# The second node mix of a spectral layer moved in front of its second weight, and two layers in one set of pools

## Chip, cores and metric

The kernel runs on one core of one Trainium2 chip. The metric is the device time of one execution in microseconds. PE is TensorE, DVE VectorE, ACT ScalarE, POOL GpSimd, SP the engine that issues the DMAs.

## What is computed

Four graph layers in a row work on `x` of 128 graphs, 64 nodes and 256 features, all in f32. Each layer takes `h = relu(layernorm(x))` and adds its result to `x`. The first mixes nodes by a normalised adjacency and has two batch norms; the second is the one that is changed; the third multiplies by the adjacency twice and ends in short recurrences over windows of nodes (LSTMs); the fourth is attention along a list of edges. The second layer, with `U` the 64 eigenvectors of the graph's Laplacian, cut to what matters:

```
_, U = jnp.linalg.eigh(L_norm)
agg = jnp.einsum('mn,bnd->bmd', U.T, features)   # first node mix, 256 features
h = jax.nn.relu(agg @ W1 + b1)                   # 256 -> 128
out = h @ W2 + b2                                # 128 -> 256
return jnp.einsum('nm,bmd->bnd', U, out)         # second node mix
```

The front of the third layer:

```
h = relu(einsum('ts,bsh->bth', adj, x @ Wg0 + bg0))
h = relu(einsum('ts,bsh->bth', adj, h @ Wg1 + bg1))
```

## The kernel before

`x` stays in SBUF as 16 blocks `X[i]` of 512 rows (8 graphs), each 128 partitions by 4 tiles by 256 features; a partition is one node of one of two graphs. `eigenvectors` finds `U` while the first layer's products run beside it, and ends by making three 128x128 block-diagonal matrices: `BDA` from the adjacency, `BDU` from `U`, `BDUT` from its transpose. Each holds the matrix twice, for the two graphs of a tile. `mix` multiplies a block by such a matrix: the tile is the stationary operand and the matrix is moved past it, 128 columns at a time, so that the result comes out transposed (features on partitions). It goes to two PSUM banks.

`layer1` is the second layer (they are counted from 0). For each block `i` it first finishes the first layer for block `i + 2` (`end0`: batch norm on ACT, transposes by `ident` on PE, residual add on DVE) and takes the norm of block `i + 1` (`norm`: statistics on DVE, a square root on ACT, seven small DVE operations, four relus on ACT). Then come the first mix by `BDU`; its copy `a`, one half on DVE and one on ACT (`move` alternates); the first weight, with the weight stationary and `a` moving in 512 columns; a relu with bias on ACT into `z`; the second weight with `z` stationary and 256 columns moving; the bias on DVE into `y`; the second mix, `BDUT` stationary and `y` moving in 512 columns; and the residual add on DVE. The last three are done twice, for two tiles each.

`layer2` is the third layer. `adjacency_layers` loads two weights and makes small tables from the biases (`w2_rs`, `w2_B`, `w2_N`, and the second bias by way of `W1`), then does for each block the norm, a copy of `X[i]` out to memory (`spilled`), mix by `BDA`, first weight, a maximum with a table on DVE, second weight, bias, mix by `BDA` and relu. Ahead of block 2 it emits `edges`, the sorted edge tables of the fourth layer, held behind what had been emitted last on DVE, ACT and PE. `windows` then runs the recurrences.

Tiles come from pools. Each stage opens its own pools (`stage`), and a pool that takes over the place of a closed one waits for it (`reuse_waits`). The second layer has PSUM pools of 3, 3 and 2 banks, the third of 4 and 2, with 2 more for `edges`. The order of instructions on an engine is not that of the source: the framework puts them in order by its own plan, in which what is emitted first has precedence and what isn't ready is overtaken. So work of neighbouring blocks is interleaved. Nearly every instruction is recorded under line 799, where a helper (`Ordered`) issues it; rows are told apart by tile names.

Of the kernel before, what the change touches and what calls it, by code (L numbers as in the profile page):

```python
# [8 lines left out]
F32 = mybir.dt.float32  # L9
I32 = mybir.dt.int32  # L10
AF = mybir.ActivationFunctionType
ALU = mybir.AluOpType
AX = mybir.AxisListType
PSUM = bass.MemoryType.PSUM
# [1383 lines left out]
B, N, D = 128, 64, 256  # L1398
P = 128
NB = 16  # L1400
TPB = 4
BT = 512
E = 512
# [17 lines left out]
class Kernel:  # L1421
# [441 lines left out]
    def end0(self, i, psum):  # L1863

        sc2, sh2 = self.affine2
        for oc in range(2):
            self.act(self.part(i, oc), self.part(i, oc), AF.Identity, scale=sc2[:, oc:oc + 1], bias=sh2[:, oc:oc + 1])
        self.add_transposed(psum, i, lambda dc, j: self.part(i, dc)[:, j * P:(j + 1) * P])

    def layer1(self):
        o, io = self.o, self.io
        cx, (w, pool, psum, ps2, ps0) = self.stage([("l1w", 1), ("l1", 2), ("l1ps", 3), ("l1bps", 3), ("l1eps", 2)])
        with cx:
            W1 = self.weights(w, "w1_1", io["L1_gnn_W1"])
            W2 = self.weights(w, "w1_2", io["L1_gnn_W2"])
            b1 = self.columns(w, "w1_b1", io["L1_gnn_b1"])
            b2 = self.everywhere(w, "w1_b2", io["L1_gnn_b2"])

            self.end0(0, ps0)
            self.end0(1, ps0)
            hs = {0: self.norm(pool, 0)}
            for i in range(NB):
                if i + 2 < NB:
                    self.end0(i + 2, ps0)
                if i + 1 < NB:
                    hs[i + 1] = self.norm(pool, i + 1)
                h = hs.pop(i)
                a = pool.tile([P, 2, BT], F32, name="a")  # L1890
                self.mix(psum, h, self.BDU, lambda dc, p: self.move(a[:, dc, :], p[:]))
                p = psum.tile([P, BT], F32, name="ps")
                for kc in range(2):
                    self.mm(p[:], W1[:, kc, :], a[:, kc, :], kc == 0, kc == 1)
                z = pool.tile([P, BT], F32, name="z")
                self.act(z[:], p[:], AF.Relu, bias=b1[:, 0:1])
                for jj in range(0, TPB, 2):
                    p = ps2.tile([P, 2, D], F32, name="pt")
                    for j in range(2):
                        self.mm(p[:, j, :], z[:, (jj + j) * P:(jj + j + 1) * P], W2[:, 0, :])  # L1900
                    y = pool.tile([P, 2, D], F32, name="y")
                    o.add(y[:], p[:], b2[:, None, :].to_broadcast([P, 2, D]))
                    p = ps2.tile([P, 2, D], F32, name="pt")
                    self.mm(p[:].rearrange("p a b -> p (a b)"), self.BDUT[:], y[:].rearrange("p a b -> p (a b)"))
                    x = self.X[i][:, jj:jj + 2, :]
                    o.add(x, x, p[:])

    def layer2(self):  # L1910
        self.adjacency_layers()
        self.windows()

    def adjacency_layers(self):
        nc, o, io = self.nc, self.o, self.io
        cx, (w, pool, psum, ps2) = self.stage([("l2w", 1), ("l2", 2), ("l2ps", 4), ("l2bps", 2)])
        with cx:
            W0 = self.weights(w, "w2_0", io["L2_gnn_Wg0"])
            W1 = self.weights(w, "w2_1", io["L2_gnn_Wg1"])
            b0 = w.tile([1, D], F32, name="w2_b0")  # L1920
            nc.sync.dma_start(b0[:], io["L2_gnn_bg0"][None, :])
            b1 = self.everywhere(w, "w2_b1", io["L2_gnn_bg1"])


            rs = w.tile([1, P], F32, name="w2_rs")
            p = psum.tile([P, BT], F32, name="ps")
            for j in range(2):
                self.mm(p[0:1, j * N:(j + 1) * N], self.ones[:N, 0:1], self.AT[:])
            o.copy(rs[:], p[0:1, 0:P])
            B0, N0 = w.tile([P, 2, P], F32, name="w2_B"), w.tile([P, 2, N], F32, name="w2_N")  # L1930
            p = psum.tile([P, BT], F32, name="ps")
            for hc in range(2):
                self.mm(p[:, hc * P:(hc + 1) * P], b0[0:1, hc * P:(hc + 1) * P], rs[:])
            o.copy(B0[:], p[:, 0:2 * P].rearrange("p (h t) -> p h t", h=2))
            o.ts(N0[:], B0[:, :, 0:N], -1.0, ALU.mult)
            p = psum.tile([P, BT], F32, name="ps")
            for kc in range(2):
                self.mm(p[:, 0:D], B0[:, kc, :], W1[:, kc, :], kc == 0, kc == 1)
            o.add(b1[:], b1[:], p[:, 0:D])
            for i in range(NB):  # L1940
                if i == 2:
                    with ExitStack() as ce:
                        epool = ce.enter_context(self.tc.tile_pool(name="l3e", bufs=1, side="right"))
                        epsum = ce.enter_context(self.tc.tile_pool(name="l3eps", bufs=1, space=PSUM))
                        nc.vector.hold, nc.scalar.hold, nc.tensor.hold = nc.vector.last, nc.scalar.last, nc.tensor.last
                        self.edges(self.w3, epool, epsum)
                        nc.vector.hold = nc.scalar.hold = nc.tensor.hold = None
                h = self.norm(pool, i)
                nc.sync.dma_start(self.spilled(i), self.X[i][:])
                a = pool.tile([P, 2, BT], F32, name="a")  # L1950
                self.mix(psum, h, self.BDA, lambda dc, p: self.move(a[:, dc, :], p[:]))
                g = pool.tile([P, 2, BT], F32, name="g")
                for hc in range(2):
                    p = psum.tile([P, BT], F32, name="ps")
                    for kc in range(2):
                        self.mm(p[:], W0[:, kc, hc * P:(hc + 1) * P], a[:, kc, :], kc == 0, kc == 1)
                    o.tt(g[:, hc, :].rearrange("p (b n) -> p b n", n=N), p[:].rearrange("p (b n) -> p b n", n=N),
                         N0[:, hc, None, :].to_broadcast([P, BT // N, N]), ALU.max)
                y = pool.tile([P, TPB, D], F32, name="y")
                for jj in range(0, TPB, 2):  # L1960
                    p = ps2.tile([P, 2, D], F32, name="pt")
                    for j in range(2):
                        for kc in range(2):
                            self.mm(p[:, j, :], g[:, kc, (jj + j) * P:(jj + j + 1) * P], W1[:, kc, :],
                                    kc == 0, kc == 1)
                    o.add(y[:, jj:jj + 2, :], p[:], b1[:, None, :].to_broadcast([P, 2, D]))
                v = self.nodes(i // 4)
                b = 8 * (i % 4)
                self.mix(psum, y, self.BDA, lambda dc, p: self.act(
                    v[:, dc, :, b:b + 8].rearrange("p n b -> p b n"), p[:].rearrange("p (b n) -> p b n", n=N), AF.Relu))  # L1970

    def windows(self):

# [185 lines left out]
    def edges(self, w, pool, psum):  # L2159


        nc, o, io = self.nc, self.o, self.io
# [22 lines left out]
        key = pool.tile([P, 4], F32, name="ed_key")  # L2185
        o.stt(key[:], col[:, 0, :], float(E), C[:], ALU.mult, ALU.add)
        rank = pool.tile([P, 4], F32, name="ed_rank")
        ps = [psum.tile([P, E], F32, name=f"ps{x}") for x in range(2)]
        for c in range(4):
            o.ts(cmp[:], row[:], key[:, c:c + 1], ALU.is_lt)  # L2190
            o.red(rank[:, c:c + 1], cmp[:], ALU.add)
# [5 lines left out]
        for x in range(2):  # L2197
            s = pool.tile([P, E], F32, name=f"ed_s{x}")
            o.copy(s[:], ps[x][:])
            srt.append(s)  # L2200
        self.OS, self.OD = (pool.tile([P, E], F32, name="ed_" + n) for n in ("OS", "OD"))
        self.S2 = w.tile([P, E], F32, name="ed_S2")
        o.ts(self.OS[:], srt[0][:], Pm[:], ALU.is_equal)
        o.ts(self.OD[:], srt[1][:], Pm[:], ALU.is_equal)
        o.add(self.S2[:], self.OS[:], self.OD[:])
        self.OST, self.ODT = (w.tile([P, 4, N], F32, name="ed_" + n) for n in ("OST", "ODT"))
        for a, y in ((self.OS, self.OST), (self.OD, self.ODT)):
            p = psum.tile([P, 4, N], F32, name="ps0")
            for c in range(4):
                nc.tensor.transpose(p[:, c, :], a[:N, c * P:(c + 1) * P], self.ident[:N, :N])  # L2210
            o.copy(y[:], p[:])
# [4 lines left out]
        o.tt(self.cont[:, 1:E], srt[0][:, 1:E], srt[0][:, 0:E - 1], ALU.is_equal)  # L2216
        o.copy(self.contr[:, 0:E - 1], self.cont[:, 1:E])

        p = psum.tile([P, E], F32, name="ps1")
        self.mm(p[:N, :], self.A[:], self.OS[:N, :])  # L2220
        ga = cmp[:N, :]
        o.mul(ga, p[:N, :], self.OD[:N, :])
        p = psum.tile([P, E], F32, name="ps0")
        self.mm(p[0:1, :], self.ones[:N, 0:1], ga)
        self.logA = w.tile([1, E], F32, name="ed_log")
        eps = pool.tile([1, 1], F32, name="ed_eps")
# [198 lines left out]
    def run(self):  # L2425
# [4 lines left out]
        with cx:  # L2430
            self.big = [pool.tile([P, 2, 4 * BT], F32, name="big") for pool in pools]
            self.eigenvectors()
            self.layer1()
            self.w3 = self.ctx.enter_context(self.tc.tile_pool(name="l3w", bufs=1, side="right"))
            self.layer2()
        self.layer3()


# [41 lines left out]
```

## Time and profile before

| | |
|---|---|
| median of 3 runs | 2398.33 us (2397.65 to 2399.54) |
| profiled execution, its own time | 2397.88 us |
| its span | 2396.1 us |
| busy in the span | PE 96%, DVE 68%, ACT 47%, POOL 0% |
| until 392.6 us | first layer and eigenvectors |
| 392.6 to 536.4 us | second layer |
| 536.4 to 736 us | third layer, up to the recurrences |
| 736 to about 1800 us | recurrences |
| to the end | fourth layer |

A row of the profile's groups gives engine, operation, output<-inputs by the program's tile names, shapes and count, then busy time, mean length, and the idle time before it with what ended it. A tile name alone isn't unique: `w` is any weight and `ps` any tile of the main PSUM pool. A product in f32 leaves two records on PE, a transpose one. The time table in stages gives the busy time of each engine in each stretch. PE's busy time is modelled at its ends, so what the engine can do is read from the distance between starts.

### The profile page before, as it was taken

What the parts mean: (1) busy time and instruction counts of PE and PEld (TensorE: products, weight loads), DVE (VectorE), ACT (ScalarE), POOL (GpSimd) and SP (SyncE); (2) the same over time, 40 slices, a digit from 0 to 9 for tenths busy, and PEclk for the clock granted to TensorE, in tenths of its full rate; (3) what the DMA queues carried; (4) which work ended last, traced back from release to release, by engine and by line L of the source; (5) the groups of instructions that cost most, each with busy time, mean ns of one, the idle gap of its engine ahead of it and who ended that gap; (6) DMA issues with size and microseconds to landing.
All of it is one profiled execution on the core that took longest, in us unless ns stands there. A gap on an engine that the chain in (4) does not pass through costs nothing.

```text
span 2396.1 us, 31996 instructions
## 1 busy us (share of the span) xinstructions
PE 2306.2 (96%) x11801; PEld 1601.4 (67%) x11801; DVE 1618.4 (68%) x4126; ACT 1137.4 (47%) x2488; POOL 2.2 (0%) x15
## 2 busy tenths in 40 slices
PE   5998997999999999999999999999999999999989
PEld 3554444656777778888999999888884444444434
DVE  6887677878536776677776676559755556656467
ACT  4675766534434564444444444335536544434321
POOL 0000000000000000000000000000000000000000
PEclk9998998999999999999999999999999999999989
DMA  5000220221001000000100002000011000000001
GB/s 159 1 1 2 70 62 22 71 72 46 1 1 36 1 18 1 1 1 1 36 1 1 1 1 71 1 1 16 1 33 38 1 5 18 14 14 18 14 14 49
DMA packets 61048, 54.78 MB, mean 23 GB/s; under 512 B 15187, under 2 KB 58708, under 8 KB 60884
## 3 DMA queue, kind: packets, MB, share of 16 engines
q1 hardware_dynamic: 60884, 52.66, 7.1%
q8 instruction: 95, 1.56, 0.3%
q14 instruction: 69, 0.57, 0.1%
HBM read 35.86 MB, written 16.78 MB: 22 GB/s over the span
## 4 chain that ended last, share of the span: by engine, by line
PE 78%; DVE 4%; ACT 1%; issue 1%; DMA 0%; ACTq 0%; DVEq 0%
PE ps L799 66%; PE pt L799 5%; PE acc L799 5%; DVE sm_m L799 1%; PE y L799 1%; DVE X L799 1%; ACT big L799 1%; DVE aw L799 0%; DMA ls_w<-in_L_gnn_Wih_t_dram 0%; DVE n_st L799 0%; ACT ls_g L799 0%; DVE g L799 0%; DVE sm_e L799 0%; DVE ls_g L799 0%; DVE ls_s L799 0%
## 5 line engine op out<-in xcount | busy, mean ns | idle before, releaser
L799 ACT ACTIVATE ls_g<-ls_g,ls_b 128x512 f32<-128x512 f32 (+4 forms) x472 | 243.0, 565 | 155.2 <-DVE ls_g L799 153.4
L799 ACT ACTIVATE ls_g<-ps,ls_b 128x256 f32<-128x256 f32 (+3 forms) x268 | 115.4, 470 | 328.5 <-PE ps L799 324.6
L799 PE MATMUL ps<-z,w 128*128 128x512 f32 x512 | 254.0, 623 | 0.0
L799 PE MATMUL ps<-big,X 128*128 128x176 f32 (+3 forms) x848 | 212.8, 366 | 1.6 <-ACT ls_z L799 1.5
L799 DVE TENSOR_TENSOR aw<-at,ed_OST 128x1024 f32<-128x1024 f32 x128 | 149.9, 1218 | 93.1 <-PE ps L799 93.0
L799 DVE TENSOR_TENSOR ls_g<-ls_z,ps 128x512 f32<-128x512 f32 (+5 forms) x256 | 146.7, 579 | 91.9 <-PE ps L799 90.4
L799 PE MATMUL ps<-ls_tx,X 128*128 128x160 f32 (+2 forms) x960 | 206.8, 326 | 1.2 <-DVE X L799 0.6
L799 PE MATMUL ps<-X,X 128*128 128x160 f32 (+1 forms) x896 | 199.0, 306 | 0.0
L799 PE MATMUL ps<-X,ls_w 128*128 128x256 f32 x640 | 190.4, 379 | 0.0
L799 PEld LDWEIGHTS ps<-ls_tx,X 128*128 128x128 f32 x960 | 161.7, 190 | 16.0 <-DVE X L799 5.6
L799 PEld LDWEIGHTS ps<-big,X 128*128 128x128 f32 x848 | 145.9, 190 | 31.6 <-issue 19.4
L799 DVE TENSOR_TENSOR X<-ls_g 128x1024 f32<-128x1024 f32 (+2 forms) x108 | 117.4, 1087 | 50.5 <-ACT ls_g L799 50.4
L799 ACT ACTIVATE r<-ps 128x512 f32<-128x512 f32 x256 | 129.4, 622 | 42.1 <-PE ps L799 42.0
L799 PEld LDWEIGHTS ps<-X,X 128*128 128x128 f32 x896 | 148.5, 190 | 0.0
L799 PE MATMUL ps<-X,ls_s 128*128 128x256 f32 x480 | 142.3, 379 | 0.0
L799 PEld LDWEIGHTS ps<-z,w 128*128 128x128 f32 x512 | 89.1, 192 | 74.2 <-issue 65.8
L799 PE MATMUL ps<-ls_tx,ls_s 128*128 128x256 f32 x464 | 134.7, 379 | 0.0
L799 PE MATMUL ps<-ls_tx,ls_w 128*128 128x256 f32 x464 | 133.3, 380 | 0.0
L799 PEld LDWEIGHTS ps<-X,ls_w 128*128 128x128 f32 x640 | 121.4, 190 | 16.8 <-DVE X L799 0.3
L799 PE MATMUL ps<-big,ls_w 128*128 128x256 f32 x464 | 131.8, 379 | 0.7 <-ACT ls_z L799 0.7
L799 PE MATMUL ps<-ed_S,Q 64*128 64x512 f32 x512 | 128.6, 617 | 1.6 <-DVE XV L799 1.3
L799 ACT ACTIVATE big<-ps 128x512 f32<-128x512 f32 x96 | 69.2, 756 | 119.5 <-PE ps L799 119.1
(512 smaller groups left out, 4046.6 us busy)
## 6 DMA issues: line engine op xcount, KB each, us to landing
X<-in_x_dram SPq DMA_DIRECT2D x32, 512.0 KB
xs<-X SPq DMA_DIRECT2D x16, 512.0 KB
X<-xs SPq DMA_DIRECT2D x16, 512.0 KB
out_dram<-X SPq DMA_DIRECT2D x32, 256.0 KB
X<-in_L_gnn_Wih_t_dram SPq DMA_DIRECT2D x4, 512.0 KB
ls_w<-in_L_gnn_Wih_t_dram SPq DMA_DIRECT2D x4, 512.0 KB
ls_w<-in_L_gnn_Whh_t_dram SPq DMA_DIRECT2D x4, 512.0 KB
w<-in_L_gnn_W_t_dram SPq DMA_DIRECT2D x2, 512.0 KB
```

The lines of the kernel that those rows point to most:

```text
L799: i = method(*a, **kw)
```

## The change

The second layer's two halves are put in another order. The first weight now has `a` stationary and the weight moving, 128 columns at a time, so its result has nodes on partitions again. The relu with bias is written as a maximum with `-b1` on DVE; the missing `+ b1` goes into a table. The second mix is applied to these 128 features, `z` stationary and `BDUT` moving in 128 columns; its result `zu`, features on partitions, is copied by ACT. The second weight follows, and one table `T` (row sums of the mix times `b1 @ W2 + b2`) is added where the bias was. The residual add is one instruction over the block's 1024 columns, from SBUF. Four new small steps at the start make `T`.

The second layer and the third, up to the recurrences, share one set of pools (PSUM 4, 2 and 2 banks). The third layer's weights are loaded ahead of the second layer's, and its bias tables are made inside the second layer's loop, at block 4. `end0` and `edges` use the same two rotating banks, named `pe`. `edges` keeps its permutation matrices in buffers that it had used before.

```diff
+    def layers12(self):
+        cx, (w, pool, psum, ps2, ps0) = self.stage([("l1w", 1), ("l1", 2), ("l1ps", 4), ("l1bps", 2), ("l1eps", 2)])
+        with cx:
+            blocks = self.mixes2(w, psum)
+            self.layer1(w, pool, psum, ps2, ps0, blocks)
+            self.w3 = self.ctx.enter_context(self.tc.tile_pool(name="l3w", bufs=1, side="right"))
+            self.layer2(pool, psum, ps2, ps0, blocks)
...
-        cx, (w, pool, psum, ps2, ps0) = self.stage([("l1w", 1), ("l1", 2), ("l1ps", 3), ("l1bps", 3), ("l1eps", 2)])
...
+        N1 = self.everywhere(w, "w1_n", io["L1_gnn_b1"])
+        b1 = self.columns(w, "w1_b1", io["L1_gnn_b1"])
+        T = self.everywhere(w, "w1_b2", io["L1_gnn_b2"])
+        o.ts(N1[:], N1[:], -1.0, ALU.mult)
+        rs = w.tile([P, 1], F32, name="w1_rs")
+        p = psum.tile([P, BT], F32, name="ps")
+        self.mm(p[:, 0:D], b1[:, 0:1].to_broadcast([P, P]), W2[:, 0, :])
+        self.mm(p[:, D:D + 1], self.BDUT[:], self.ones[:, 0:1])
+        o.copy(rs[:], p[:, D:D + 1])
+        o.add(T[:], p[:, 0:D], T[:])
+        o.ts(T[:], T[:], rs[:], ALU.mult)
...
+            if i == 4:
+                tables()
...
-                p = psum.tile([P, BT], F32, name="ps")
+            p = psum.tile([P, TPB, P], F32, name="ps")
+            for j in range(TPB):
                 for kc in range(2):
-                    self.mm(p[:], W1[:, kc, :], a[:, kc, :], kc == 0, kc == 1)
-                z = pool.tile([P, BT], F32, name="z")
-                self.act(z[:], p[:], AF.Relu, bias=b1[:, 0:1])
-                for jj in range(0, TPB, 2):
-                    p = ps2.tile([P, 2, D], F32, name="pt")
-                    for j in range(2):
-                        self.mm(p[:, j, :], z[:, (jj + j) * P:(jj + j + 1) * P], W2[:, 0, :])
-                    y = pool.tile([P, 2, D], F32, name="y")
-                    o.add(y[:], p[:], b2[:, None, :].to_broadcast([P, 2, D]))
-                    p = ps2.tile([P, 2, D], F32, name="pt")
-                    self.mm(p[:].rearrange("p a b -> p (a b)"), self.BDUT[:], y[:].rearrange("p a b -> p (a b)"))
-                    x = self.X[i][:, jj:jj + 2, :]
-                    o.add(x, x, p[:])
+                    self.mm(p[:, j, :], a[:, kc, j * P:(j + 1) * P], W1[:, kc, :], kc == 0, kc == 1)
+            g = pool.tile([P, 2, BT], F32, name="g")
+            z, zu = g[:, 0, :].rearrange("p (t c) -> p t c", c=P), g[:, 1, :]
+            o.tt(z, p[:], N1[:, None, :].to_broadcast([P, TPB, P]), ALU.max)
+            p = psum.tile([P, BT], F32, name="ps")
+            for j in range(TPB):
+                self.mm(p[:, j * P:(j + 1) * P], z[:, j], self.BDUT[:])
+            self.act(zu, p[:], AF.Copy)
+            y = pool.tile([P, TPB, D], F32, name="y")
+            for jj in range(0, TPB, 2):
+                p = ps2.tile([P, 2, D], F32, name="pt")
+                for j in range(2):
+                    self.mm(p[:, j, :], zu[:, (jj + j) * P:(jj + j + 1) * P], W2[:, 0, :])
+                o.add(y[:, jj:jj + 2, :], p[:], T[:, None, :].to_broadcast([P, 2, D]))
+            x = self.X[i][:]
+            o.add(x, x, y[:])
...
-        ps = [psum.tile([P, E], F32, name=f"ps{x}") for x in range(2)]
+        ps = [psum.tile([P, E], F32, name="pe") for x in range(2)]
...
-        self.OS, self.OD = (pool.tile([P, E], F32, name="ed_" + n) for n in ("OS", "OD"))
+        self.OS, self.OD = (pool.tile([P, E], F32, name="ed_perm", bufs=2) for _ in range(2))
```

`mixes2` holds the loads of `adjacency_layers` and returns its table step as `tables`; the new `layer2` is its loop over blocks, otherwise unchanged.

## The prediction

> **What bounds the kernel now.** I read the share table first (PE 96%, DVE 68%), then the busy time of each engine by stage, then the order of time in one block of the second layer and at the hand-over to the third. The busy time of TensorE is modelled at its ends, so I took stage bounds from busy times and TensorE's work from the distance between starts. By stage (stretch, length, then busy microseconds and count of PE, PE's weight loads, DVE, ACT, POOL; granted clock; DMA share; GB/s):
>
> ```profile
> 395.80:405.00 9.20, 6.18 (x30) 4.60 (x29) 8.68 (x32) 7.70 (x13) 0.00 (x0) 0.69 0.25 43
> 426.00:507.00 81.00, 80.88 (x399) 56.29 (x398) 69.44 (x205) 38.44 (x75) 0.00 (x0) 1.00 0.20 66
> 528.00:536.40 8.40, 5.32 (x15) 2.22 (x13) 3.39 (x6) 0.69 (x1) 0.00 (x0) 1.00 0.19 62
> 536.40:542.80 6.40, 3.44 (x13) 2.63 (x13) 5.61 (x31) 1.75 (x5) 0.00 (x0) 0.55 0.58 185
> 542.80:560.00 17.20, 16.64 (x81) 11.96 (x80) 16.36 (x75) 10.26 (x23) 0.00 (x0) 0.97 0.19 63
> 600.00:710.00 110.00, 108.17 (x543) 79.54 (x542) 52.98 (x164) 45.97 (x77) 0.00 (x0) 1.00 0.00 1
> 395.80:536.40 140.60, 134.26 (x636) 92.42 (x634) 113.03 (x353) 73.77 (x140) 0.00 (x0) 0.97 0.19 60
> ```
>
> The reader is to see three things. From 426 to 507 us, ten blocks of the second layer, PE never stands still, but DVE is already at 86%. From 528 to 542.8 us PE is half empty: the second layer drains, then the third starts from nothing, at half clock. From 600 us, in the third layer, PE is full and DVE at 48%.
>
> One block in order of time, PE alone (start us, length us, engine, line of the helper, operation, output<-inputs, count). ident,big is a transpose of the first layer's output, BDU,h the first node mix, a,w the first weight, w,z the second weight, y,BDUT the second mix:
>
> ```profile
> 441.08 0.93 PE L799 MATMUL pt<-ident,big 128*128 128x128 f32 x7
> 442.02 1.13 PE L799 MATMUL pt<-w,z 128*128 128x256 f32 x4
> ...
> 443.10 1.28 PE L799 MATMUL ps<-BDU,h 128*128 128x128 f32 x10
> 444.21 1.02 PE L799 MATMUL pt<-y,BDUT 128*128 128x512 f32 x2
> 445.07 1.03 PE L799 MATMUL pt<-w,z 128*128 128x256 f32 x4
> 445.94 0.83 PE L799 MATMUL ps<-BDU,h 128*128 128x128 f32 x6
> 446.61 1.02 PE L799 MATMUL ps<-a,w 128*128 128x512 f32 x2
> ...
> 450.12 1.13 PE L799 MATMUL pt<-w,z 128*128 128x256 f32 x4
> ```
>
> From 442.02 to 450.12 is one block: 8.10 us. From start to next start, a 128-column record costs 0.111 us (443.10 to 444.21, ten), a 256-column one 0.218, a 512-column one 0.43, a transpose 0.134. Every f32 product leaves two records (160 for the 80 products of ten blocks), a transpose one.
>
> The hand-over:
>
> ```profile
> 534.54 1.13 PE L799 MATMUL pt<-y,BDUT 128*128 128x512 f32 x2 [0.78 <-DVE y L799]
> ...
> 536.51 0.38 PE L799 MATMUL ps<-AT,ones 64*1 64x64 f32 x4 [0.85 <-DVE X L799]
> ...
> 539.23 1.19 PE L799 MATMUL ps<-w_rs,w_b 1*128 1x128 f32 x4 [2.33 <-DVE n_r L799]
> ...
> 542.80 2.45 PE L799 MATMUL ps<-BDA,h 128*128 128x128 f32 x16
> ...
> 545.81 3.70 PE L799 MATMUL ps<-a,w 128*128 128x512 f32 x8 [0.56 <-DVE a L799]
> ```
>
> The first table product waits until the last residual add has freed the old pools, and the first mix of the third layer comes at 542.80. Its 16 records end by about 544.7, the next product starts at 545.81: one more gap of about 1.1 us. So I count the third layer as running without a break from 543.9.
>
> **What the Trainium skill says.** "Perfetto Trace Analysis", Identifying the Most-Contended Engine, calls matmul busy share a poor measure: here PE reads 97% busy in 542.8 to 560 with that 1.1 us gap inside, so it agrees. "VectorE: DVE Perf Modes", The perf-mode tier table, gives a two-tensor f32 operation one element per cycle in SBUF as in PSUM, so the merged residual add is not cheaper per element. The forms agree: 1223 ns for 1024 elements in SBUF (X<-ls_g), 684 for 512 out of PSUM (y<-pt,w_b). "TensorE: Matmul & The Clock Gate", What's actually happening, has the clock halve after an idle window: granted clock 0.55 in 536.4 to 542.8.
>
> **The change, part by part.**
>
> *TensorE, second layer.* Before, a block costs 8 transposes (1.07), first mix 16 records (1.78), first weight 4 of 512 columns (1.72), second weight 8 of 256 (1.74), second mix 4 of 512 (1.72): 8.03, measured 8.10. After, the first weight is 8 products of 128 columns (16 records, 1.78) and the second mix 4 of 128 (8 records, 0.89): 1.07 + 1.78 + 1.78 + 0.89 + 1.74 = 7.26. Saved: 0.77 a block, 12.3 in sixteen.
>
> *VectorE, second layer.* 113.03 busy in 395.8 to 536.4 is 7.06 a block. Two residual adds out of PSUM go (they follow each other at about 0.61: each is 0.08 shorter in spacing than in length), one maximum over 512 columns out of PSUM comes (0.61), one residual add over 1024 columns in SBUF comes (1.22 less 0.08 = 1.14). Net +0.53: 7.59 a block, 121.5 in all. **DVE becomes the longer of the two**, 7.59 against 7.26; the PE saving can't be had in full.
>
> *ScalarE.* A relu out of PSUM (687 ns) becomes a copy out of PSUM (about 595, the row of a<-ps). ACT is at 47% there: nothing.
>
> *New tables at the start.* Two products, then four small or 256-wide DVE operations, about 1.0 us of DVE. They wait for the second weight, whose load now has four issues of the third layer ahead of it on SP's queue: the two weight issues took 1.46 together and the two biases about 0.4 each, so 2.3 us later, plus some 640 KB in front. The first weight itself isn't needed before 408.9, sixteen us after the queue opens: covered by the transposes, norms and first mix. The new sums could hold PE or DVE in front of the first blocks by 0 to 4 us; the trace doesn't show it, a gain has no source. I take 1, as DVE is 94% busy there with work that can go first.
>
> *Third layer's tables inside block 4.* 1.8 us of PE (under DVE's bound now, so free), 1.3 us of DVE (copy 0.26, copy 0.43, scale 0.19, add 0.42), counted below. If DVE weren't the bound, they would cost 1.8 on PE.
>
> *Shared pools.* Nothing has to drain: norm, mix and first product of the third layer's blocks 0 and 1 may stand in the gaps of the second layer's last blocks. *Edge tables* on two rotating PSUM banks instead of two named ones, and on permutation buffers used again: same banks in number, each re-used only after a read that already precedes it; 0, within half a us either way, under the third layer's products.
>
> *Sum.* DVE work until the last residual add: 121.5 + 1.0 + 1.3 = 123.8. Where DVE is the limit today it reaches 94% (8.68 of 9.20) and 95% (16.36 of 17.20); at 94.5% it takes 131.0, from 395.8 to 526.8. The third layer's first norm (2.9 us of DVE: four statistics at 0.35, four aggregates at 0.10, seven small operations) fits mostly beside the last block's PE chain; with its relu (2.06 on ACT) the third layer runs without a break from about 529.5, against 543.9: 14.4 gained. Less 1 for the start: **13.4**. The third layer is PE-bound and only moves, and what follows moves with it. The profiled execution took 2397.9 (span 2396.1 and 1.8 around it), the median of the runs shown is 2398.3, 0.4 above; I forecast 2385.0.
>
> What is late next in the second layer: the maximum on DVE. The second mix waits for it, where before a relu on idle ACT stood; queued behind it on DVE are statistics and residual adds of later blocks, up to 1.2 us each.
>
> **Rivals.**
> *PE stays the bound.* If norms and table work run far enough ahead, DVE always has its next input and a block goes at PE's pace: 8.10 to 7.33 saves 12.3, and the hand-over, 543.9 less 528.0 with 1.8 of tables kept, some 10 to 14. For it: DVE ran ahead at the start. Against: 7.59 over 7.26. About 2375.
> *Only the hand-over is gained.* DVE waits for PE and PE for DVE in turn and the block stays at 8.1: the gap of 9 goes, less start and leftover bubble of 3: about 2392.
> *Slower: DVE as the alternating bound.* The chain of a block now crosses DVE up to four times (copy of one mixed half, maximum, add, residual), all in one queue. If DVE keeps today's 86% (69.44 of 81.0), a block takes 7.59/0.86 = 8.83: 11.7 lost in sixteen against 9 gained at the hand-over; with a start penalty of 4, 6.7 slower, 2405. It decides from a block of about 8.8 us on. Against it: DVE's 86% is today's because PE was the bound, not DVE's limit.
> *The change doesn't do what it says.* If the order issued keeps the third layer's first norm behind the second layer's end, the bubble stays though the pools are shared: the gain is block time alone, 0 to 4: about 2396.
>
> **How the numbers follow.** A measurement of this kernel can tell about 0.2%, 4.8 us, from no change. The DVE-bound forecast has 0.53 (2379 to 2390), PE-bound 0.14 (2371 to 2379), hand-over alone 0.15 (2390 to 2394), no bubble filled 0.07 (2394 to 2401), slower 0.11. Faster 0.82, same 0.07, slower 0.11. The range 2374 to 2397 leaves out three eighths of the PE-bound case (0.05), the slow case (0.11) and over half of the unfilled one (0.04): 0.20.
>
> **What would show it.** Right: in the second layer DVE at 94% or more over ten blocks and PE's starts with gaps; a block of 7.9 to 8.1 us; the first mix of the third layer on PE before 531; no half-clock stretch near it. Wrong: PE still without a gap at 7.3 us a block (PE-bound); a block over 8.5 us with DVE under 90% (the alternating wait); a first mix of the third layer after 538; or a start of the first mix of the second layer after 408, where it was 405.3.

## The result and the profile after

The changed kernel takes 2397.57 us (median of 22 runs, 2394.66 to 2400.38), beside 2400.25 us (22 runs) for the kernel before on the same chip: ratio 0.9987 [0.9981, 0.9993], 2.7 us. That is less than 0.2%. The forecast was 13.4 us.

Profiled alone, the two are even: the span after is 2396.8, before 2396.1. The execution of after was already 3.0 us late ahead of the changed part, 2.3 of them because the clock was halved there (last section). So I count from a mark at the start of the changed part: the DVE copy that fills the node mix BDU, at 393.8 us before and 396.75 after. From that copy to the third layer's second BDA mix it is 160.16 us before and 159.78 after.

The busy times by stretch; the steady blocks are shown in two parts, and the last row runs from the mark to the second layer's last residual add (length, then busy us and count of PE, PE's weight loads, DVE, ACT, POOL; granted clock; DMA share; GB/s):

```profile
450.00:480.00 30.00, 29.04 (x216) 26.34 (x216) 28.43 (x100) 13.33 (x28) 0.00 (x0) 1.00 0.19 63
480.00:507.00 27.00, 23.95 (x170) 21.67 (x168) 23.92 (x75) 10.39 (x23) 0.00 (x0) 1.00 0.18 60
528.00:536.40 8.40, 7.09 (x53) 6.46 (x51) 6.44 (x22) 3.61 (x8) 0.00 (x0) 1.00 0.33 107
536.40:543.70 7.30, 5.99 (x43) 5.36 (x42) 5.34 (x18) 2.59 (x6) 0.00 (x0) 1.00 0.33 106
600.00:710.00 110.00, 108.17 (x549) 79.67 (x548) 52.49 (x164) 46.68 (x77) 0.00 (x0) 1.00 0.00 1
396.75:547.40 150.65, 132.83 (x931) 119.92 (x932) 129.98 (x440) 78.08 (x154) 0.00 (x0) 0.96 0.22 69
```

The bubble of 528 to 542.8 us is gone: PE is busy for 84 and 82% of those stretches, where it was half empty, and the clock stays full. But the reason isn't that the third layer moved forward; those stretches are still the second layer. The third layer's first mix comes at 543.73, where it was 542.80. DVE is at 95% in 450 to 480, as forecast, and at 89% in 480 to 507; over the whole last row it is 86%. The third layer at 600 to 710 is as before.

Now PE's order of time, the view that decided the case. `w,a` is the first weight, `BDUT,g` the second mix, `w,g` the second weight, `BDU,h` the first mix of the next block, `ident,big` a transpose. The bracket is the idle time ahead of a row and what ended it:

```profile
466.10 0.39 PE L799 MATMUL ps<-w,a 128*128 128x128 f32 x2
466.32 0.60 PE L799 MATMUL pe<-ident,big 128*128 128x128 f32 x4
466.95 1.83 PE L799 MATMUL ps<-w,a 128*128 128x128 f32 x14
468.62 0.60 PE L799 MATMUL pe<-ident,big 128*128 128x128 f32 x4
469.56 1.16 PE L799 MATMUL ps<-BDUT,g 128*128 128x128 f32 x8 [0.35 <-DVE g L799]
...
526.43 1.16 PE L799 MATMUL ps<-BDUT,g 128*128 128x128 f32 x8 [0.79 <-DVE g L799]
527.43 1.06 PE L799 MATMUL ps<-BDU,h 128*128 128x128 f32 x8
528.34 1.99 PE L799 MATMUL pt<-w,g 128*128 128x256 f32 x8
530.17 1.05 PE L799 MATMUL ps<-BDU,h 128*128 128x128 f32 x8
531.06 0.39 PE L799 MATMUL ps<-w,a 128*128 128x128 f32 x2
531.97 1.83 PE L799 MATMUL ps<-w,a 128*128 128x128 f32 x14 [0.52 <-ACT a L799]
534.58 1.16 PE L799 MATMUL ps<-BDUT,g 128*128 128x128 f32 x8 [0.78 <-DVE g L799]
...
543.73 1.06 PE L799 MATMUL ps<-BDA,h 128*128 128x128 f32 x8
```

From 526.43 to 534.58 a block takes 8.15 us with no transpose in it. Its 48 records are worth 6.19 us by the spacings used in the forecast (1.78 + 1.78 + 0.89 + 1.74). Of the other 1.96 us, 1.75 lie in two places, and both are round trips: a result leaves PE, another engine copies or changes it, and PE needs it back. The second half of the mix ends just ahead of the first weight, so the weight waits for ACT's copy of that half into `a`; from start to start this costs 0.69 us. Then the second mix waits for the maximum on DVE (`g`), and this costs 1.06. (The brackets, 0.52 and 0.78, count from the modelled end of the row before, and are smaller.) PE keeps to its order while it waits: ACT had finished `h` for the next first mix at 517.57, but its products start only behind the second mix, at 527.43.

In the upper rows the same block has eight transposes, and they lie exactly in these two places; the wait shrinks to 0.35 and the block still takes 8.09 (the next second mix starts at 477.65). The intervals between starts of the second mix say it for the whole layer: 7.99 to 8.03 with twelve transposes, 8.03 to 8.15 with eight, 8.09 to 8.15 with none (longer are only the first, 8.72, and the one with the third layer's tables, 11.21). The blocks with twelve prove little, as their own records are worth 7.80; those with eight (7.26) and none (6.19) show that the length doesn't follow the work. Before, a block with eight took 8.10 and the last two, with none, 7.45.

From the copy of BDU to the third layer's second mix, taking the first row of each block's first mix, the 0.4 us come out as a sum of three:

| | before | after | difference |
|---|---|---|---|
| copy of BDU to the first mix | 11.46 | 13.67 | +2.2 |
| fifteen block intervals | 116.2 | 125.2 | +9.0 |
| last block's mix to the third layer's second mix | 32.5 | 20.9 | -11.6 |

The 9.0 are: the first two blocks (8.13 + 8.72 against 6.43 + 6.66), 3.8; the two blocks with the third layer's tables (13.0 + 6.24 against two ordinary ones of 8.05), 3.1; the last two (8.15 each against 6.09 + 7.45), 2.8; the rest -0.7. The middle blocks didn't move, though each has 0.77 us less for PE to do.

These 0.4 us leave most of the 2.7 us unplaced. From the third layer's second BDA mix to its last one it is 179.1 us after and 180.2 before, so from the copy of BDU to there the gain is 1.5 us (338.9 against 340.3). Behind that the source is the same, and the two profiled executions differ by another 0.7 us; in all twelve profiles this last part lies between 1658.5 and 1662.0 us, so the rest of the 2.7 can't be placed.

### The profile page after: what moved, and what is told of

Same layout as the page of the kernel before. It is cut to its first block, busy times and chain, and to the rows that moved or that the text cites. A ratio compares the mean times of both kernels' runs of the same rounds, so it can differ in the third digit from the quotient of the medians.

```text
span 2396.8 us, 32517 instructions
## 1 busy us (share of the span) xinstructions
PE 2299.8 (96%) x12061; PEld 1623.3 (68%) x12061; DVE 1622.3 (68%) x4130; ACT 1135.8 (47%) x2488; POOL 2.2 (0%) x15
## 4 chain that ended last, share of the span: by engine, by line
PE 76%; DVE 5%; ACT 1%; issue 1%; DMA 0%; SPq 0%; ACTq 0%; DVEq 0%
PE ps L799 66%; PE acc L799 5%; PE pt L799 4%; DVE sm_m L799 1%; PE y L799 1%; DVE X L799 1%; PE pe L799 1%; DVE g L799 1%; ACT ls_g L799 0%; DVE aw L799 0%; DVE n_st L799 0%; ACT L799 0%; DMA w_b<-in_L_gnn_b_dram 0%; ACT a L799 0%; DMA ls_w<-in_L_gnn_Wih_t_dram 0%
```

## Experiments

Two theories stood after the result. *DVE*: its 7.6 us of work a block, at 95%, set the 8.1 us. *Chain*: the order in which products are issued leaves two round trips open, whatever DVE's load. A further question was what the start and the third layer's tables cost; experiments 5, 6 and 10 are about it.

**1. The new order of products alone, in the old pools** (PSUM 4, 2 and 2 banks; the third layer as before).

```diff
-        cx, (w, pool, psum, ps2, ps0) = self.stage([("l1w", 1), ("l1", 2), ("l1ps", 3), ("l1bps", 3), ("l1eps", 2)])
+        cx, (w, pool, psum, ps2, ps0) = self.stage([("l1w", 1), ("l1", 2), ("l1ps", 4), ("l1bps", 2), ("l1eps", 2)])
```
and the body of `layer1` as in the change.

> The kernel before with the second layer's new order of products alone (table T at its start, PSUM pools 4, 2 and 2 banks), in pools of its own, so that the third layer still starts behind it. Two theories of why the changed kernel gained only 3 us where 13 were forecast. Chain theory: PE issues in order, and in each block of the new second layer two round trips stand open in that order (mix half to copy to first weight; first weight to maximum on DVE to second mix), so a block stays at 8.1 us although PE has 0.8 us less to do, and the drain is no shorter; then this kernel loses the start (1 to 3 us) and gains nothing: 0 to 5 us slower than before, blocks of 8.0 to 8.2 us. DVE theory: the block is bound by DVE's 7.6 us of work at 94 to 95%: 8.0 us where norms are still to be done, and under 7.5 us in the last three blocks, where they are not; the kernel is within 2 us of before.

Measured: 2407.83 us, ratio 1.0035 [1.0021, 1.0049], some 8 us slower than before, more than either theory had said. From the copy of BDU to the third layer's second mix it is 6.5 us longer: 1.5 at the start and 5.9 in the fifteen intervals, less 0.9 at the end. Blocks 8.38, 8.51, then 7.99 to 8.22; last block's mix to the third layer's first 21.0 us, as before (21.3). So the new order by itself is a loss, and its blocks keep 8.1 where no third layer shares the buffers.

**2. The shared pools alone, with the old order of products** (tables at block 4, loads as in the change).

```diff
-            p = psum.tile([P, TPB, P], F32, name="ps")
...
+            p = psum.tile([P, BT], F32, name="ps")
+            for kc in range(2):
+                self.mm(p[:], W1[:, kc, :], a[:, kc, :], kc == 0, kc == 1)
+            z = g[:, 0, :]
+            self.act(z, p[:], AF.Relu, bias=b1[:, 0:1])
```
and the old second half behind it.

> The changed kernel with the second layer's old order of products put back (first weight stationary, relu on ACT, second mix last), in the shared pools, with the third layer's loads first and its tables at block 4; the second layer's two-bank pool has 2 banks where it had 3. Both theories: the hand-over is the part that gains, about 10 to 12 us, as PE goes on without the stretch of 14.8 us in which it had some 8 us of work; the block itself stays at 8.1 us, or gets up to 0.3 longer by the bank less (5 us in all). 4 to 11 us faster than before, so faster than the whole change. If it is no faster than before, the gain of the hand-over isn't due to the pools.

Measured: 2391.09 us, ratio 0.9965 [0.9952, 0.9979], 8.8 us faster, and 8.7 from the copy of BDU to the third layer's second mix. The copy to the first mix takes 11.2 us, the third layer's first mix comes at 534.6. The gain of the change is here, and the new order takes most of it back: 8 lost and 8.8 gained leave about one, and 2.7 was measured, which the intervals (some 3 us to either side) allow.

**3. DVE's largest step nearly removed.** The residual add works on 64 of 1024 columns, so this kernel leaves out most of the layer's result.

```diff
-            x = self.X[i][:]
-            o.add(x, x, y[:])
+            o.add(x[:, 0, 0:64], x[:, 0, 0:64], y[:, 0, 0:64])
```

> The changed kernel, with the second layer's residual add cut to 64 of 1024 columns (the layer's result is thereby left out of x but for those columns): about 1.0 us less of DVE work in a block, nothing else changed. DVE theory: the block falls from 8.05 to about 7.3 us (PE's 7.26 is then the limit). Chain theory: the block stays at 8.0 to 8.15 us, DVE's busy share falls from 95% to about 82% in 450 to 480 us, and the end moves by less than 3 us.

Measured: one run, 2395.03 us. Busy times by stretch (columns as above), and PE's order:

```profile
450.00:480.00 30.00, 28.52 (x209) 26.07 (x207) 25.39 (x91) 11.49 (x25) 0.00 (x0) 1.00 0.18 60
480.00:507.00 27.00, 22.30 (x158) 20.25 (x158) 16.03 (x62) 12.00 (x25) 0.00 (x0) 1.00 0.21 72
```

```profile
528.87 1.83 PE L799 MATMUL ps<-w,a 128*128 128x128 f32 x14 [0.52 <-ACT a L799]
531.48 1.16 PE L799 MATMUL ps<-BDUT,g 128*128 128x128 f32 x8 [0.78 <-DVE g L799]
...
539.63 1.16 PE L799 MATMUL ps<-BDUT,g 128*128 128x128 f32 x8 [0.79 <-DVE g L799]
```

DVE falls from 89% to 59% in 480 to 507 (4.2 of the 7.9 us are the removed adds; most of the rest are norm statistics that fall outside this stretch here), and from the second mix at 531.48 to that at 539.63 it is 8.15 us, as in the changed kernel; the waits are the same to the hundredth. In 450 to 480, where DVE was at 95%, it is now at 85%, and the blocks there are no shorter (8.03 to 8.15). The DVE theory falls. That "DVE g" stands in the bracket names where the round trip goes, not an engine that is full.

**4. The next block's first mix issued behind this block's maximum**, in the changed kernel, so that it stands between the first weight and the second mix.

```diff
+        def first(i):
+            h = hs.pop(i)
+            a = mixed[i] = pool.tile([P, 2, BT], F32, name="a")
+            self.mix(psum, h, self.BDU, lambda dc, p: self.move(a[:, dc, :], p[:]))
+        first(0)
...
-            h = hs.pop(i)
-            a = pool.tile([P, 2, BT], F32, name="a")
-            self.mix(psum, h, self.BDU, lambda dc, p: self.move(a[:, dc, :], p[:]))
+            a = mixed.pop(i)
...
             o.tt(z, p[:], N1[:, None, :].to_broadcast([P, TPB, P]), ALU.max)
+            if i + 1 < NB:
+                first(i + 1)
```

> The changed kernel with one thing moved in the source: the first mix of block i+1 and its copies are emitted behind the maximum of block i, in front of its second mix, so that PE has 1.8 us of products between the first weight and the second mix, and the second mix and second weight between the mix and the next first weight. Same instructions. Chain theory: the two round trips are covered, a block falls to DVE's 7.6 to 7.8 us while norms are to be done and to 6.3 to 7.3 us at the end: 5 to 10 us faster than the changed kernel, 8 to 13 faster than before. DVE theory: no block under 8.0 us before the last three, at most 3 us faster than the changed kernel.

Measured: 2386.74 us, ratio 0.9949 [0.9936, 0.9963], by the two ratios some 9 us faster than the changed kernel. PE's order:

```profile
485.11 1.72 PE L799 MATMUL ps<-w,a 128*128 128x128 f32 x14
486.68 1.95 PE L799 MATMUL ps<-BDU,h 128*128 128x128 f32 x16
488.46 1.06 PE L799 MATMUL ps<-BDUT,g 128*128 128x128 f32 x8
```

Both halves of the next mix, 1.78 us of work, now cover the maximum, and the second mix starts without a wait, here and in every block from 450 to 510 us. The chain theory had said so; nothing but the order of emission was changed. The blocks average 7.63 us instead of 8.34, but go in turns of 6.3 to 10.3, since the transposes bunch: 20 in the longest, none in the shortest. That 7.63 is close to DVE's work for a block, which asks whether DVE has become the bound.

**5. The order of the start**, in the changed kernel: the second layer's loads first on the queue, and the four steps of `T` behind the first norm.

```diff
-            blocks = self.mixes2(w, psum)
-            self.layer1(w, pool, psum, ps2, ps0, blocks)
+            blocks = self.layer1(w, pool, psum, ps2, ps0)
```
with `mixes2` called in `layer1` behind its own loads, and the norm of block 0 ahead of the steps of `T`.

> The changed kernel with its start alone changed: the second layer's loads are issued ahead of the third layer's, and the four steps that make T are emitted behind the first norm instead of in front of the first transposes. In the changed kernel's profile the first mix comes 13.7 us after the copy of BDU, where it was 11.5 before; with T alone (the reorder alone) it was 13.0, with the third layer's loads in front but no T (the pools alone) 11.3. So T's steps, standing in DVE's and PE's order while their loads are under way, are the cost, and the loads in front add 0.7. Expected: 11.3 to 12 us from copy to first mix, 1.5 to 2.5 us faster than the changed kernel (4 to 6 faster than before). If the distance stays over 13, DVE's additional work and not the wait is the cost.

Measured: 2392.75 us, ratio 0.9965 [0.9951, 0.9979]. In its profile the copy to the first mix takes 10.71 us instead of 13.67, and the copy to the third layer's second mix 157.12 instead of 159.78: 2.7 us. By the two ratios the gain over the changed kernel is 0.0022, some 5 us, with an interval that reaches down to 2; I take the profile's number. The reason can be read in the changed kernel's start, PE and DVE in order of time:

```profile
402.88 0.23 DVE L799 TENSOR_SCALAR w_n<-w_n 128x128 f32<-128x128 f32 x1 [0.15 <-DMA w_n<-in_L_gnn_b_dram]
403.83 0.67 PE L799 MATMUL ps<-w,w_b 128*128 128x256 f32 x2 [1.05 <-DMA w_b<-in_L_gnn_b_dram]
405.88 0.42 DVE L799 TENSOR_TENSOR w_b<-ps,w_b 128x256 f32<-128x256 f32 x1 [1.07 <-DMA w_b<-in_L_gnn_b_dram]
...
410.42 2.77 PE L799 MATMUL ps<-BDU,h 128*128 128x128 f32 x12
```

Three steps of `T` wait for their loads, and what stands behind them on PE and DVE comes later. With the loads first, the product of `w,w_b` comes 5.4 us after the copy instead of 7.1.

**6. The third layer's tables in three pieces**, at blocks 4, 6 and 8, in the changed kernel.

```diff
-            if i == 4:
-                tables()
+            if i in (4, 6, 8):
+                tables[i // 2 - 2]()
```

> The changed kernel with the third layer's bias tables made in three pieces, at blocks 4, 6 and 8, instead of in one go at block 4. In one go two blocks take 19.2 us together where 16.1 are usual, and 17.8 against 16.2 with the old order of products. If the cost is the chain of three products with a DVE copy between each (each holding one of four banks and PE's order), the pieces hide: those blocks take 8.0 to 8.5 us each and the kernel is 2 to 3.5 us faster than the changed one. If it is the work itself (1.8 us of PE, 1.3 of DVE), the loss is spread over the three blocks and less than 1 us is won.

Measured: 2396.57 us (21 runs), ratio 0.9986 [0.998, 0.9993], the same as the changed kernel; intervals average 8.34 in both. So what the tables cost isn't that three dependent steps stand together.

**7. Experiments 3 and 4 together**: the next mix ahead, the residual add on 64 columns.

> The kernel with the mix ahead, with the second layer's residual add cut to 64 of 1024 columns (the layer's result is left out of x but for those), 1.0 us less of DVE work a block. With the mix ahead the blocks average 7.6 us and DVE is at 92 to 97%. If the chain was what hid DVE's bound, DVE's bound now shows: the average falls to 6.8 to 7.3 us (PE's 7.26 with transposes, 6.3 without). If the chain still sets the pace, it stays at 7.5 us or more, as the same cut left the changed kernel at 8.1.

Measured: one run, 2378.87 us. The blocks come to 7.43 us in the middle and average 7.28. The same removal that gave nothing in experiment 3 now takes 0.35 a block. In 450 to 510 us PE's busy time rises from 57.3 us in experiment 4 to 59.3, and DVE's falls from 55.4 to 52.8. With the round trips covered, DVE's work did hold the blocks back; now PE's does.

**8. Experiment 4 with both copies into `a` on ACT.**

```diff
-            self.mix(psum, h, self.BDU, lambda dc, p: self.move(a[:, dc, :], p[:]))
+            self.mix(psum, h, self.BDU, lambda dc, p: self.act(a[:, dc, :], p[:], AF.Copy))
```

> The kernel with the mix ahead, with both copies of the first mix on ACT in the second layer (one of the two was on DVE): 0.61 to 0.68 us less of DVE work a block, 0.6 more on ACT, which is under half busy there. DVE-bound: blocks of 7.0 to 7.3 us on average instead of 7.6, 4 to 6 us faster than the kernel with the mix ahead, 15 to 18 faster than before. If ACT's own queue (relus of the next norm, 2.06 us at a stretch, in front of the copies) delays the first weight more than DVE gains, the average stays at 7.6 or rises.

Measured: 2381.03 us, ratio 0.9914 [0.9901, 0.9928], 19 us faster than before; the intervals average 7.25 us. PE's order of one block, and the stretch (columns as above):

```profile
481.39 1.95 PE L799 MATMUL ps<-w,a 128*128 128x128 f32 x16
483.17 1.95 PE L799 MATMUL ps<-BDU,h 128*128 128x128 f32 x16
484.96 1.06 PE L799 MATMUL ps<-BDUT,g 128*128 128x128 f32 x8
485.85 0.82 PE L799 MATMUL pe<-ident,big 128*128 128x128 f32 x6
486.76 1.99 PE L799 MATMUL pt<-w,g 128*128 128x256 f32 x8
488.59 0.38 PE L799 MATMUL pe<-ident,big 128*128 128x128 f32 x2
488.81 1.95 PE L799 MATMUL ps<-w,a 128*128 128x128 f32 x16
```

```profile
450.00:510.00 60.00, 59.36 (x452) 55.45 (x451) 54.16 (x171) 32.55 (x65) 0.00 (x0) 1.00 0.21 71
```

From 481.39 to 488.81 it is 7.42 us, and no row waits for another engine. A block with eight transposes takes 7.43, one with none 6.31: here the length follows the work, unlike in the changed kernel. That is 0.17 over the 7.26 that the forecast gave for PE's work.

**9. Experiments 5 and 8 together.**

> The mix ahead, both copies on ACT and the changed start (second layer's loads first, T behind the first norm), together. The causes are apart from each other: copy of BDU to first mix 10.7 us instead of 12.9, blocks of 7.43 us in the middle as with the copies on ACT (PE's bound with transposes), so 2 to 4 us faster than that kernel: 2376 to 2380, 20 to 24 us under before. If the start's gain is lost again behind DVE's or ACT's own work in the first three blocks, within 1.5 us of it.

Measured: 2375.59 us (4 runs, 2375.42 to 2378.16), beside 2398.59 for the kernel before: ratio 0.9905 [0.9888, 0.9921], 23 us faster. The copy to the third layer's second mix takes 139.03 us instead of 159.78. The copy to the first mix takes 11.3 us, where 10.7 was expected. By the ratios it can't be told from experiment 8 (0.9905 against 0.9914, each with 0.0015 or so to either side); by the profiles it is 3.7 us shorter from the copy of BDU to the third layer's second mix (139.03 against 142.72). It is faster than the kernel before and than the changed one.

**10. Experiment 9 with the tables at block 14**, where a drain of the second layer might have had room.

```diff
-            if i == 4:
+            if i == 14:
```

> The same with the third layer's bias tables made at block 14 instead of block 4. At block 4 two blocks take 16.3 us where 14.9 are usual, although the tables' products are 1.8 us of PE. If the cost is PE time in a stage that is bound by PE, moving it gains nothing: within 1.5 us of the kernel with all three edits. If it is the wait of the tables' chain, it falls into the blocks without transposes and norms, where PE waits anyway: 1 to 2 us faster. It may also be late for the third layer's first block, which needs the table after its first weight: then 1 to 3 us slower.

Measured: 2377.60 us, ratio 0.9906 [0.9889, 0.9922]: no different from experiment 9. The long interval moved along with the tables (9.82 at the end, where it was 10.1 at block 4), and from the copy of BDU to the third layer's second mix it is 140.41 us against 139.03. This fits the reading that, where blocks are bound by PE's work, the tables cost their own PE time wherever they stand; it doesn't rule out a small wait.

## Why the prediction was wrong

**The sign was right, the size wrong by 10.7 us**: 2.7 gained, 13.4 forecast. The sign is partly luck: one half of the change lost 8 us (experiment 1), the other gained 8.8 (experiment 2), and the forecast expected no loss from the first. Nearest in number is the case "the change doesn't do what it says", about 2396, by accident, as its reason, a bubble that stays, isn't there. Nearest in mechanism is the rival "only the hand-over is gained": "DVE waits for PE and PE for DVE in turn and the block stays at 8.1". The trace shows such waits, for ACT and for DVE. This rival gave 2392 because it took start and bubble together for 3, and the first, the last and the table blocks for nothing.

*Where it failed.* The step "DVE becomes the longer of the two" made the slower engine's work the length of a block, and the sum then packed all of DVE's work at 94.5%. DVE's work was sized well (28.43 us in 30, 7.6 a block, against 7.59), and so was PE's. What failed is the inference that one of them must then be full. The block is 8.0 to 8.15 with DVE at 95% and at 59% (experiment 3), and with eight or no transposes on PE: the two round trips set it. The last residual add came at 547.4 us, where 526.8 was forecast; 3 us of that are this execution's late start. From the mark to that add DVE is at 86%, since its first and last blocks can't run as dense as its middle ones; in 536.4 to 543.7 it is at 73%.

*Signs that were met for another reason.* The forecast's pace, 7.59 / 0.945 = 8.03 us a block, and its sign of being right, "a block of 7.9 to 8.1 us", nearly agree with the measured 8.03 to 8.15, and so does DVE's 93% over 426 to 507 us with its "94% or more over ten blocks". That is luck: in experiment 3 the same pace stays with less DVE work. The sign that told was "a first mix of the third layer after 538": it came at 543.73, or 540.8 without this execution's late start.

*What I had in hand.* The forecast did name the wait: "the maximum on DVE. The second mix waits for it, where before a relu on idle ACT stood." It priced it only by what is queued on DVE, not by the time in which PE has nothing to issue while the result travels. The price stood in the forecast's own view of the hand-over: the second mix at 534.54, with no other work left to cover it, waits 0.78 us for DVE. In the changed kernel the wait for the maximum is the same 0.78 in the blocks without transposes, and that for the copy of `a` ahead of it 0.52. In the kernel before, a block of the middle has 0.01 us of gaps on PE, its relu and copies included: that cover went with the old order. The Trainium skill's "Perfetto Trace Analysis", Optimization Strategy, tells the reader to look for the gaps on the engine that matters and for what releases them. For gaps that repeat, it offers too few buffers as one possible reason; here experiment 4 adds no buffer and changes only the place of one group of instructions, and the wait for `g` goes.

*Term by term.* PE saves 0.77 a block: right, but turned into waiting time, and had only when the chain was opened (experiment 8: 8.1 to 7.43). Start: 1 forecast of 0 to 4, 2.2 measured; the cover that I named, DVE work that can go first, isn't taken, since later steps stand behind those that wait for loads. The check in the forecast, a first mix after 408, was met (410.4, of which 3 are the late start). Tables at block 4: "under DVE's bound now, so free", 3.1 measured. Splitting them gave nothing, and moving them, tried in experiment 9's kernel alone, gave nothing. The first two blocks and the last two: not priced at all, 3.8 and 2.8. Before, the last two intervals were 6.09 and 7.45, as they hold no transposes; blocks that are set by round trips don't get shorter for that. Hand-over: forecast as one term of 14.4 with the blocks; by itself 11.6 measured. A small misreading: the gap at 545 us was counted as 1.1 us at full-clock spacing, but the first four of the sixteen records ran at half clock and the last starts at 544.98, so it is some 0.7. And where the forecast takes from the Trainium skill's "TensorE: Matmul & The Clock Gate", What's actually happening, that the clock halves after an idle window, the trace of before has it at half from 537.0 us on, when no gap on PE in the hand-over had yet been longer than 0.85 us; a whole idle window is not what it shows there. Shared pools without a drain, and ScalarE at nothing: no run speaks against either.

*The other cases.* "PE stays the bound" is what experiments 8 and 9 reach, and 9 took 2375.6, where that rival said 2375; but it takes another order, ACT's copies and another start. "DVE as the alternating bound", slower, saw the right kind of wait; its block of 8.83 isn't there, and of all versions only the new order alone (experiment 1) was slower than before. "The bubble stays" is excluded by the stretches after the change and by experiment 2.

*What stays open.* Why, in the changed kernel, the second half of the next block's first mix is issued behind the second weight, just ahead of the first weight that needs it, and not earlier, was not settled; moving the emission moves it (experiment 4), and that is all that is shown. Nor is it known why the tables cost 3.1 us in the changed kernel, where PE waits anyway, against 1.8 of PE work.

## What to carry to other kernels

When products are put in another order, write down for one block in which order PE will issue them and, for each result that goes through another engine and comes back, what PE has to do meanwhile. Each return with nothing behind it costs the whole round trip. Here the waits were 0.5 and 0.8 us in the blocks without transposes; in those with eight the transposes filled most of the two gaps, but the block was no shorter. The engines' busy shares don't show it: DVE stood at 95% and looked like the bound. The test is whether a block gets shorter when it has less to do. So first emit the next block's first products between a result and its use; only then is it worth asking which engine is full.

## What was not expected of the hardware

The granted clock halved for 6.8 us at 373.3 us in the profiled execution of after, in the first layer, where before had none and PE's rows stand in the same order. PE had been idle for 3.37 us just ahead of that stretch in both executions. Fourteen records of one kind took 8.69 us there:

```profile
375.25 8.69 PE L799 MATMUL ps<-z,w 128*128 128x512 f32 x14
```

In the execution of before the same fourteen took 6.28. The same stretch, or half of it, was there in seven of the ten experiments, and not in 3, 7 and 9. It makes 2.3 us here between single executions of kernels whose first layers run alike, most of the gain that was to be measured, so stretches are compared from a mark that lies behind it. What decides whether it comes was not looked for.
